# Conditioned attention on one core: one head's softmax sums in two chunks move from ScalarE to VectorE, one addition of q's corner block from VectorE to GpSimd

## The chip, the cores and the metric

The kernel runs on one core of a Trainium2 chip. The core has five engines that run side by side: TensorE (PE in the profile, PEld for its weight loads), VectorE (DVE), ScalarE (ACT), GpSimd (POOL) and SyncE (SP), which issues most transfers. Each engine works through its own instructions in program order and waits at semaphores for the others. The metric is the device time of one execution in microseconds (us), the median of several; lower is better.

## The reference

The input x has 8 sequences of 512 rows and 512 columns, with one conditioning row for each sequence. Attention has 16 heads of 32 columns:

```python
Q = split(x @ Wq.T + bq); K = split(x @ Wk.T + bk); V = split(x @ Wv.T + bv)
cQ = Q + split(cond @ Wq.T + bq)
cK = K + split(cond @ Wk.T + bk)
scores = einsum('bhqd,bhkd->bhqk', cQ, cK) / sqrt(32)
attn = softmax(scores, axis=-1)
out  = x + merge(einsum('bhqk,bhkd->bhqd', attn, V))
```

Everything is float32. The softmax needs, for each head and query row, the maximum of its 512 scores, the exponentials, and their sum.

## The kernel before

**Tiles and steps.** A tile t is one sequence and four heads: 8 sequences by 4 groups make T = 32 tiles. The main loop `for t in range(1, T - 3)` takes one tile a step, and each step has four items, in this order: "V" (i = 0), "q" (1), "k" (2) and "v" (3). A 512-row sequence is cut into four query chunks of 128, numbered qc.

Two tiles are always under way. The softmax of tile t + 1 is prepared in step t: its row scores for chunk 1, 2 and 3 in items V, q and k, and chunk 0 of tile t + 2 in item v (`rows`). In item V, `weighted` multiplies the exponentials of tile t - 1 with V. In items q, k and v, `products` computes a quarter of the next sequence's q, k or v projections.

**Odd and even tiles.** Tiles 1, 3, ..., 27 are in the list `BLOCKED`. For an odd tile the exponentials are computed once, with queries in the partitions, kept in `arena` (`rows_kept`), exchanged between partitions by transfers (`exchange`, L677, some issued by GpSimd, the others by SyncE) and turned by VectorE (`turn_blocks`, L666). For an even tile they are computed twice: once in the PSUM banks only for the sums (`denominators`, L693), and once more in the other orientation (`exponentials`, L749 to L763). So an even step has, in each item, four exponentials by L763 for tile t and four by L693 for tile t + 1, which is odd. An odd step has L693 alone. The exponential of L693 subtracts the row maximum, which it gets as a bias (`nmax`, from VectorE, L602 and L655), and returns the sum of its row in `sums`. In the profile this is a second instruction, ACTIVATION_READ_ACCUMULATOR, behind the ACTIVATE. Later `masked` (L801, GpSimd) spreads the sums for the division in `weighted`.

**The projections** use seven products instead of eight for a 2 by 2 block scheme. An odd step calls `four_products`, an even step `three_products`; each writes to two PSUM banks, `one_` and `two_`. The results of a pair of tiles lie in `c1` (with its second half `c12`) and `c2` (with its second half `c22`). In the odd step, ScalarE takes the four products out of PSUM (L540, L542, L543; L527 and L532 for v) and GpSimd adds them up (L544, L545). In the even step VectorE adds the other three in three operations (L556, L557, L558). `c12` is the corner block: it gets two products there, the others one each.

**The order of the work** is written out by hand (`manual_schedule`): each engine's order is the order of the program. The eight PSUM banks change their roles at every item; `begin` and `released` keep a list of them by the time at which they come free. In an even step the exponentials of an item take the first four, the row scores the last four. So the row scores (L646) of item k go to the two banks of heads 2 and 3 of item q's sums, which L693 frees, and to `one_` and `two_` of item q, which L557 and L558 free. Those of item v stand in the same way to item k. SyncE's and GpSimd's transfers are issued at the places that `ORDERS` names.

Of the kernel before, what the change touches and what calls it, by code (L numbers as in the profile page):

```python
# [11 lines left out]
AF = mybir.ActivationFunctionType  # L12
ALU = mybir.AluOpType
AX = mybir.AxisListType
# [3 lines left out]
def kernel(  # L18
# [38 lines left out]
    nc = tc.nc  # L57
    P = 128
# [10 lines left out]
    HS = S // 2  # L69
# [2 lines left out]
    EARLY = 3  # L72
    SINGLY = "qk"
    BY_POOL = (3,)
    WARM = (48, 4)
    BLOCKED = list(range(1, T - 4, 2))

# [44 lines left out]
    def banks(i, n=1):  # L122

        row = row_of[0] or [at_end[j] for j in TURNS[turn[0]]]
        j = row[i]
        if n == 1:
            return psum[:, j, :]
        k = row[i + 1]
        return psum[:, j : k + 1 : k - j, :]
# [14 lines left out]
    def released(*roles):  # L144
        order[:] = [row_of[0][i] for i in roles]
# [76 lines left out]
    def rows_kept(t, half):  # L222

        a = arena[:, half * HG : (half + 1) * HG, :]
        return a.rearrange("p g (c h s) -> p g c h s", c=2, h=HG)
# [104 lines left out]
    def in_place(b):  # L330
# [5 lines left out]
    wT = {  # L336
        n: const.tile([P, NC, D], F32, tag=f"wT{n}", name=f"wT_{n}") for n in ("q", "k", "v")
    }
# [63 lines left out]
    def pair_of(t, n):  # L402

        if (n, t // 2) not in pairs:
            pairs[n, t // 2] = qkp.tile([P, 2, S], F32, tag=n, name=f"{n}T_{t // 2}")
        return pairs[n, t // 2]
# [66 lines left out]
    def twice(a):  # L473
        return a.unsqueeze(1).broadcast_to([P, 2, HS])

    def halves(a):
        return a.rearrange("p (h s) -> p h s", h=2)


    def parts_of(n, b, u):  # L480

        if n == "v":
            v = vs[b % 2]
            return v[:, u::2, :HS], v[:, u + 2, :HS], v[:, u::2, HS:], v[:, u + 2, HS:]
        o = pair_of(b * G + u * 2, n)
        return halves(o[:, 0, :]), o[:, 0, HS:], halves(o[:, 1, :]), o[:, 1, HS:]

    def plus(n, b, u, g, o, pt, rest):

        if n == "v":  # L490
            nc.vector.tensor_tensor(o, pt, rest, ALU.add)
        else:
            add = tok[:, "qk".index(n), u * 2 + g, b : b + 1]
            nc.vector.scalar_tensor_tensor(o, pt, add, rest, ALU.add, ALU.add)

    def first_products(n, b, u, dens, small, at, first=0, held=None):
# [17 lines left out]
        nc.vector.tensor_tensor(c1[:, 0, :], two_[:, HS:], m1, ALU.add)  # L514
        plus(n, b, u, 1, c22, one_[:, HS:], c12)

    def four_products(n, b, u, dens, small, at):

        one_, two_ = banks(at), banks(at + 1)
        c1, c12, c2, c22 = parts_of(n, b, u)  # L520
        m1 = c2[:, 0, :]
        if n == "v":
            v = vs[b % 2].rearrange("p c (two f) -> p (c two) f", two=2)
            product(n, b, u, 1, one_[:, :HS])
            product(n, b, u, 6, one_[:, HS:])
            dens(range(EARLY))
            nc.scalar.copy(v[:, u * 2 + 1 : u * 2 + 5 : 3, :], halves(one_))  # L527
            dens(range(EARLY, HG))
            small()
            product(n, b, u, 2, two_[:, :HS])  # L530
            product(n, b, u, 7, two_[:, HS:])
            nc.scalar.copy(v[:, u * 2 : u * 2 + 6 : 5, :], halves(two_))  # L532
        else:
            dens()
            product(n, b, u, 1, one_[:, :HS])
            product(n, b, u, 6, two_[:, HS:])
            small()
            product(n, b, u, 2, two_[:, :HS])
            product(n, b, u, 7, one_[:, HS:])
            nc.scalar.copy(m1, one_[:, :HS])  # L540
            i = "qk".index(n)
            nc.scalar.activation(c1, halves(two_), AF.Identity, bias=tok[:, i, u * 2, b : b + 1])  # L542
            nc.scalar.activation(c22, one_[:, HS:], AF.Identity, bias=apart_tok[:, i, u, b : b + 1])  # L543
        nc.gpsimd.tensor_tensor(c1, c1, twice(m1), ALU.add)  # L544
        nc.gpsimd.tensor_tensor(c22, c22, c12, ALU.add)  # L545

    def three_products(n, b, u, dens, small, at):

        dens()
        one_, two_ = banks(at[0]), banks(at[1])  # L550
        product(n, b, u, 5, one_[:, HS:])
        product(n, b, u, 4, one_[:, :HS])
        small()
        product(n, b, u, 3, two_[:, :HS])
        c1, c12, c2, c22 = parts_of(n, b, u)
        nc.vector.tensor_tensor(c12, one_[:, HS:], c12, ALU.add)  # L556
        nc.vector.tensor_tensor(c2, halves(one_), twice(c22), ALU.add)  # L557
        nc.vector.tensor_tensor(c12, two_[:, :HS], c12, ALU.add)  # L558
        if n != "v":
            for g in range(2):  # L560
                qkT[n, b * G + u * 2 + g] = pair_of(b * G + u * 2, n)[:, g, :]
# [32 lines left out]
    sums = {}  # L594
# [73 lines left out]
    def exchange(t, half):  # L668
# [3 lines left out]
        for g in range(HG):  # L672
            for a in range(HG):
                queue = nc.gpsimd if a in BY_POOL else nc.sync
                of = arena[a * BL : (a + 1) * BL, half * HG + g, :]
# [3 lines left out]
    def denominators(t, qc, w=HG, js=range(HG)):  # L679

        if t >= T - 2:
            return
        for j in js:
            if t in BLOCKED:
                to = rows_kept(t, qc // 2)[:, :, qc % 2, j, :].rearrange(
                    "p g (c e) -> p g c e", e=BL
                )
            else:
                to = banks(w + j)
            of = banks(w + j)  # L690
            if t in BLOCKED:
                of = of.rearrange("p (c g e) -> p g c e", g=HG, e=BL)
            nc.scalar.activation(  # L693
                to,
                of,
                AF.Exp,
                bias=nmax[t][:, qc, j, :],
                accum_out=sums[t][:, qc, j, :],
            )

    def split_max(t, on=nc.gpsimd):

# [169 lines left out]
    apart_tok = const.tile([P, 2, NC // 2, B], F32, tag="aparttok", name="aparttok")  # L872
# [39 lines left out]

    keep_warm(WARM[0])
    bank = bank_of
# [22 lines left out]
    project(0, "k", pk, two[0])  # L937
    keep_warm(WARM[1])
    turn_first_x(1)
# [174 lines left out]
    def turn_more(t, i):  # L1114

        for u in (t - 1, t, t + 1):
            if u in BLOCKED and (t - u, i) in TURNED:
                n = turned.get(u, 0)
                turned[u] = n + TURNED[t - u, i]
                turn_blocks(u, range(n, turned[u]))  # L1120

    ORDERS = {
        (1, 0): [],
        (1, 1): ["store", "x"],
# [8 lines left out]
    for t in range(1, T - 3):  # L1133
        b, r = divmod(t, G)
        blocks = t in BLOCKED
        w = 0 if blocks else HG
        items = ["V", "q", "k", "v"]
        for i, item in enumerate(items):
            rows = (t + 1, i + 1) if i < 3 else (t + 2, 0)
            begin(w)  # L1140
            if not blocks:
                exponentials(t, i)
            late_first = item in ("v" if blocks else "qkv") and t % 2 == 1
            hold = row_max(*rows, late_first, w, not blocks and item in SINGLY)

            def held(i=i, hold=hold):
                hold()
                if i == 2:
                    split_max(t + 1)
                    turn_max(t + 1)  # L1150

            dens = lambda js=range(HG): denominators(*rows, w, js)
            if item in "qkv":
                products(t, item, blocks, held, dens, nothing)
            else:
                held()
                dens()
                if blocks:
                    weighted(t - 1, banks(4), banks(5), nothing)
                    released(6, 7, 0, 1, 2, 3, 5, 4)  # L1160
                else:
                    weighted(t - 1, banks(0), banks(1), nothing)
                    released(2, 3, 1, 4, 5, 6, 7, 0)
            if i == 0 and r % 2 == 0:
                turn_x(t + NC + 2)
                turn_x(t + NC + 3)
            if i == 0 and r == 1:
                combine_x(b + 1, 1, nc.gpsimd)
            if i == 1 and r == 0:
                combine_x(b + 1, 0, nc.gpsimd)  # L1170
            if i == 2:
                aparts[t] = masked(t)
            turn_more(t, i)
            for what in ORDERS[t % 2, i]:
                if what == "store":
                    store()
                elif what == "residual":
                    if 3 < t + 1 <= T - 4:
                        load_residual(t + 1)
                elif what == "x":  # L1180
                    load_pairs()
                elif t + 1 in BLOCKED:
                    exchange(t + 1, what)
# [67 lines left out]
    t = T - 3  # L1251
# [25 lines left out]
    t = T - 2  # L1277
# [25 lines left out]
    t = T - 1  # L1303
# [61 lines left out]
    b, g = divmod(t, G)  # L1365
# [55 lines left out]
```

## Time and profile before

| | |
|---|---|
| median of 3 runs | 660.53 us (660.41 to 660.67) |
| the profiled execution | 660.98 us, span 658.9 us |
| TensorE's granted clock | 1.00 |
| PE busy | 651.5 us, 99% of the span |
| VectorE busy | 574.6 us, 87% |
| ScalarE busy | 542.5 us, 82% |
| GpSimd busy | 336.8 us, 51% |
| one odd and one even step in the middle | 18.58 + 20.46 us |

The span runs from the first to the last instruction of the execution that was profiled; that execution's own time is 2 us longer. Busy times of one engine are sums over its instructions. A matmul that waits for a semaphore after the one before it has begun may show as a gap, or only as a group of matmuls that takes longer than its like, because matmuls overlap and their ends are modelled. Rows of the order of time give the start in us from the span's beginning, the length, engine, line, operation, output and input, shapes and count, and in brackets how long the engine stood idle before and what ended that. "PEld" rows are weight loads, which run ahead of their matmuls.

### The profile page before, as it was taken

What the parts mean: (1) busy time and instruction counts of PE and PEld (TensorE: products, weight loads), DVE (VectorE), ACT (ScalarE), POOL (GpSimd) and SP (SyncE); (2) the same over time, 40 slices, a digit from 0 to 9 for tenths busy, and PEclk for the clock granted to TensorE, in tenths of its full rate; (3) what the DMA queues carried; (4) which work ended last, traced back from release to release, by engine and by line L of the source; (5) the groups of instructions that cost most, each with busy time, mean ns of one, the idle gap of its engine ahead of it and who ended that gap; (6) DMA issues with size and microseconds to landing.
All of it is one profiled execution on the core that took longest, in us unless ns stands there. A gap on an engine that the chain in (4) does not pass through costs nothing.

```text
span 658.9 us, 23947 instructions
## 1 busy us (share of the span) xinstructions
PE 651.5 (99%) x9568; PEld 304.1 (46%) x9568; DVE 574.6 (87%) x844; ACT 542.5 (82%) x1393; POOL 336.8 (51%) x446
## 2 busy tenths in 40 slices
PE   8999999999999999999999999999999999999997
PEld 7444443544535454444445444454553544444432
DVE  4898989989798898979989898898979888897886
ACT  2579798888989888898989979788897988889664
POOL 5552543647537464466635664464753646444340
PEclk9999999999999999999999999999999999999999
DMA  9718548385675838657484875839567582940212
GB/s 205 144 44 214 118 109 210 67 220 122 153 172 121 209 74 214 149 130 194 94 214 97 191 155 131 210 71 217 118 164 166 115 205 48 223 106 4 56 33 33
DMA packets 140818, 90.91 MB, mean 138 GB/s; under 512 B 117436, under 2 KB 126308, under 8 KB 140708
## 3 DMA queue, kind: packets, MB, share of 16 engines
q1 hardware_dynamic: 133252, 73.91, 49.0%
q0 software_dynamic: 5568, 14.95, 8.8%
q8 instruction: 75, 1.23, 0.8%
q10 hardware_dynamic: 1888, 0.52, 0.4%
q14 instruction: 35, 0.29, 0.1%
HBM read 20.27 MB, written 8.39 MB: 43 GB/s over the span
## 4 chain that ended last, share of the span: by engine, by line
PE 95%; POOL 2%; DVE 1%; DMA 1%; issue 0%; ACT 0%; ACTq 0%; DVEq 0%; POOLq 0%
PE psum L469 43%; PE psum L774 17%; PE psum L646 10%; PE psum L638 9%; PE psum L752 8%; PE psum L749 3%; PE psum L410 2%; DMA early<-in_x_dram 1%; PE psum L1227 1%; PE psum L1340 0%; PE psum L811 0%; ACT psum L693 0%; POOL wc_q L364 0%; POOL wc_q L361 0%; POOL wc_k L362 0%
## 5 line engine op out<-in xcount | busy, mean ns | idle before, releaser
L602 DVE TENSOR_REDUCE nmax<-psum 128x1 f32<-128x512 f32 x326 | 204.9, 680 | 41.7 <-PE psum L646 38.2
L693 ACT ACTIVATE psum<-psum,nmax 128x512 f32<-128x512 f32 x256 | 169.2, 665 | 46.5 <-DVE nmax L602 34.3
L763 ACT ACTIVATE arena<-psum 128x512 f32<-128x512 f32 x264 | 136.3, 603 | 29.3 <-PE psum L752 21.7
L693 ACT ACTIVATE arena<-psum,nmax 128x512 f32<-128x512 f32 x224 | 152.8, 709 | 5.8 <-issue 4.4
L666 DVE STREAM_TRANSPOSE blocks<-blocks 128x1024 f32<-128x1024 f32 x112 | 132.2, 1218 | 0.2 <-issue 0.2
L655 DVE TENSOR_REDUCE nmax<-psum 128x2 f32<-128x1024 f32 x87 | 105.3, 1212 | 1.1 <-PE psum L646 1.1
L842 POOL TENSOR_TENSOR res<-res,recs 128x512 f32<-128x512 f32 x30 | 31.4, 1048 | 121.1 <-DVE res L841 121.1
L677 POOL DMA_DIRECT2D blocks<-arena x112 | 55.9, 504 | 72.3 <-ACT arena L693 63.5
L646 PE MATMUL psum<-kT,qT 32*128 32x512 f32 x576 | 87.9, 604 | 0.0
L774 PE MATMUL psum<-arena,v 128*32 128x512 f32 x576 | 68.5, 597 | 0.0
L752 PE MATMUL psum<-qT,kT 32*128 32x512 f32 x528 | 67.9, 587 | 0.0
L638 PE MATMUL psum<-kT,qT 32*64 32x512 f32 x896 | 62.4, 613 | 0.0
L646 PEld LDWEIGHTS psum<-kT,qT 32*128 32x128 f32 x576 | 37.6, 182 | 34.1 <-DVE kT L558 6.5
L693 ACT ACTIVATION_READ_ACCUMULATOR psum<-psum,nmax 128x1 f32 x256 | 52.4, 205 | 0.0
L774 PE MATMUL psum<-blocks,v 128*32 128x256 f32 x896 | 52.1, 381 | 0.0
L693 ACT ACTIVATION_READ_ACCUMULATOR arena<-psum,nmax 128x1 f32 x224 | 50.9, 227 | 0.0
L843 POOL TENSOR_TENSOR xr<-res,xr 128x512 f32<-128x512 f32 x30 | 38.4, 1281 | 2.4
L209 POOL TENSOR_TENSOR xr<-xr,wT_q 128x512 f32<-128x512 f32 x30 | 38.3, 1280 | 0.3
L774 PEld LDWEIGHTS psum<-blocks,v 128*32 128x32 f32 x896 | 26.3, 110 | 25.0 <-ACT arena L763 10.6
L841 DVE STREAM_TRANSPOSE res<-psum 128x512 f32<-128x512 f32 x28 | 20.1, 717 | 19.0 <-issue 16.0
L469 PE MATMUL psum<-wT_v,xT 128*32 128x256 f32 x512 | 34.2, 382 | 0.0
L469 PE MATMUL psum<-wc_v,xc 128*32 128x256 f32 x512 | 33.5, 379 | 0.0
(194 smaller groups left out, 1012.3 us busy)
## 6 DMA issues: line engine op xcount, KB each, us to landing
blocks<-arena SPq DMA_DIRECT2D x336, 128.0 KB, 4.1
blocks<-arena POOLq DMA_DIRECT2D x112, 128.0 KB, 4.0
xr<-in_x_dram SPq DMA_DIRECT2D x60, 128.0 KB, 2.8
x<-in_x_dram SPq DMA_DIRECT2D x56, 128.0 KB, 2.8
out_dram<-xr SPq DMA_DIRECT2D x56, 128.0 KB, 2.3
w_q<-in_L_cond_Wq_dram SPq DMA_DIRECT2D x4, 256.0 KB
w_k<-in_L_cond_Wk_dram SPq DMA_DIRECT2D x4, 256.0 KB, 8.2
w_v<-in_L_cond_Wv_dram SPq DMA_DIRECT2D x4, 256.0 KB
```

The lines of the kernel that those rows point to most:

```text
L469: nc.tensor.matmul(pt[r], still[:, r], moving, start=(kc == kcs[0]), stop=(kc == kcs[-1]))
L602: nc.vector.tensor_reduce(nmax[t][:, qc, j : j + 1, 0], pt, AX.X, ALU.max, negate=True)
L638: nc.tensor.matmul(pt[i * n : (i + 1) * n], qkT["q", t][r, qc * P + i * n : qc * P + (i + 1) * n], qkT["k", t][r, :], start=True, stop=True,)
L646: nc.tensor.matmul(pt, qkT["q", t][r, qc * P : (qc + 1) * P], qkT["k", t][r, :], start=True, stop=True,)
L655: nc.vector.tensor_reduce(nmax[t][:, qc, pr * 2 : pr * 2 + 2, 0], pt, AX.X, ALU.max, negate=True)
L666: nc.vector.transpose(e, e)
L677: queue.dma_start(to.rearrange("p c h s -> p (c h s)"), of)
L693: nc.scalar.activation(to, of, AF.Exp, bias=nmax[t][:, qc, j, :], accum_out=sums[t][:, qc, j, :],)
L752: nc.tensor.matmul(bank[j], qkT["k", t][r, kc * P : (kc + 1) * P], qkT["q", t][r, :], start=False, stop=True,)
L763: nc.scalar.activation(e[:, i, :], bank[pr * 2 + i], AF.Exp)
L774: nc.tensor.matmul(pt[j * HD : (j + 1) * HD, at], vs[b % 2][:, kc, (g * HG + j) * HD : (g * HG + j + 1) * HD], e, start=(kc == chunks[0]), ...
L843: nc.gpsimd.tensor_tensor(xr[t], y, xr[t], ALU.add)
```

## The change

Two things are done, both in the main loop.

First, `BY_VECTOR` names head 0 in chunks 2 and 3. For odd tiles from 3 on, the exponential of that head and chunk (L693) is issued without its sum. A new function, `sums_by_vector`, adds the row up with a VectorE reduction over the 512 exponentials in the arena. It reads them as four pieces of 128 a row. It is called at the end of items q (chunk 2) and k (chunk 3) of the even steps, behind VectorE's work on the item's products (`SUMMED`). These are 13 even steps and 26 reductions.

Second, for q alone (`HELPED`), the corner block is summed in another order. In the odd step ScalarE writes its term for the corner to an unused part of q's weight buffer (`room_beside`, two pieces of 128 columns a row) instead of `c22`, and GpSimd's addition writes the sum to `c12` instead of `c22`. In the even step VectorE computes `c2` first, then the third product minus that term into the weight buffer, and GpSimd adds `c22` to it. So VectorE has two operations there instead of three, and GpSimd one more: 14 even steps. The sum is the same.

TensorE's and SyncE's instructions and their order stay as they were.

```diff
+    BY_VECTOR = {2:(0,),3:(0,)}
+    HELPED = "q"
...
+    def room_beside(n):
+        a = wT["q" if n == "q" else "k"][:, 0:2, 3 * P :]
+        return a if n in HELPED else None
+
+    def split_of(a):
+        return a.rearrange("p (c s) -> p c s", c=2)
...
-            nc.scalar.activation(c22, one_[:, HS:], AF.Identity, bias=apart_tok[:, i, u, b : b + 1])
+            nc.scalar.activation(
+                beside if n in HELPED else c22,
+                split_of(one_[:, HS:]) if n in HELPED else one_[:, HS:],
+                AF.Identity,
+                bias=apart_tok[:, i, u, b : b + 1],
+            )
         nc.gpsimd.tensor_tensor(c1, c1, twice(m1), ALU.add)
-        nc.gpsimd.tensor_tensor(c22, c22, c12, ALU.add)
+        if n in HELPED:
+            nc.gpsimd.tensor_tensor(split_of(c12), beside, split_of(c12), ALU.add)
+        else:
+            nc.gpsimd.tensor_tensor(c22, c22, c12, ALU.add)
...
-        nc.vector.tensor_tensor(c12, one_[:, HS:], c12, ALU.add)
-        nc.vector.tensor_tensor(c2, halves(one_), twice(c22), ALU.add)
-        nc.vector.tensor_tensor(c12, two_[:, :HS], c12, ALU.add)
+        if n in HELPED:
+            beside = room_beside(n)
+            nc.vector.tensor_tensor(c2, halves(one_), twice(c12), ALU.add)
+            nc.vector.tensor_tensor(beside, split_of(two_[:, :HS]), beside, ALU.subtract)
+            nc.gpsimd.tensor_tensor(split_of(c12), beside, split_of(c22), ALU.add)
+        else:
+            nc.vector.tensor_tensor(c12, one_[:, HS:], c12, ALU.add)
+            nc.vector.tensor_tensor(c2, halves(one_), twice(c22), ALU.add)
+            nc.vector.tensor_tensor(c12, two_[:, :HS], c12, ALU.add)
...
+            by_scalar = t not in BLOCKED or t == 1 or j not in BY_VECTOR.get(qc, ())
             nc.scalar.activation(
...
-                accum_out=sums[t][:, qc, j, :],
+                **({"accum_out": sums[t][:, qc, j, :]} if by_scalar else {}),
             )
+
+    def sums_by_vector(t, qc):
+
+        if t in BLOCKED:
+            for j in BY_VECTOR[qc]:
+                nc.vector.tensor_reduce(
+                    sums[t][:, qc, j, :],
+                    rows_kept(t, qc // 2)[:, :, qc % 2, j, :],
+                    AX.XY,
+                    ALU.add,
+                )
...
+    SUMMED = {1:[2],2:[3]}
...
             turn_more(t, i)
+            if not blocks:
+                for qc in SUMMED.get(i, ()):
+                    sums_by_vector(t + 1, qc)
```

More of the change, by code (lines that the diff above doesn't have):

```diff
@@ L555, in three_products @@
         c1, c12, c2, c22 = parts_of(n, b, u)
-        nc.vector.tensor_tensor(c12, one_[:, HS:], c12, ALU.add)
-        nc.vector.tensor_tensor(c2, halves(one_), twice(c22), ALU.add)
-        nc.vector.tensor_tensor(c12, two_[:, :HS], c12, ALU.add)
+        if n in HELPED:
+            beside = room_beside(n)
+            nc.vector.tensor_tensor(c2, halves(one_), twice(c12), ALU.add)
[5 more added lines that the diff above has]
+            nc.vector.tensor_tensor(c12, two_[:, :HS], c12, ALU.add)
         if n != "v":
```

## The prediction

> **What bounds the kernel now.** I read the page's first and fourth parts, then the chain that ended last inside one pair of steps, the busy times of that pair item by item, and the order of time of ACT, PE's weight loads, DVE and POOL there. The profiled execution took 660.98 us with a span of 658.9; the median of the runs is 660.53, 0.07% less. All savings below are so small that they carry over to the median as they are.
>
> ```profile
> span 658.9 us, 23947 instructions
> PE 651.5 (99%) x9568; PEld 304.1 (46%) x9568; DVE 574.6 (87%) x844; ACT 542.5 (82%) x1393; POOL 336.8 (51%) x446
> PE 95%; POOL 2%; DVE 1%; DMA 1%; issue 0%; ACT 0%; ACTq 0%; DVEq 0%; POOLq 0%
> ```
>
> PE is busy throughout and holds 95% of the chain. So freeing DVE, ACT or POOL is worth only what PE loses by waiting for them, and a busy PE can hide such a wait in a matmul that begins late. It shows in one pair of steps, cut into the odd step and the even step's items V, q, k, v (columns: PE, PEld, DVE, ACT, POOL busy, then clock, DMA share, GB/s):
>
> ```profile
> 221.32:239.90 18.58, 18.58 (x300) 7.86 (x304) 18.16 (x24) 15.07 (x42) 10.11 (x13) 1.00 0.69 165
> 239.90:245.74 5.84, 5.84 (x97) 3.00 (x100) 4.84 (x7) 5.53 (x14) 3.25 (x3) 1.00 0.09 18
> 245.74:250.51 4.77, 4.77 (x72) 2.37 (x76) 4.60 (x8) 3.88 (x11) 3.77 (x5) 1.00 0.48 106
> 250.51:255.59 5.08, 5.08 (x73) 2.54 (x76) 4.05 (x9) 5.04 (x14) 0.80 (x3) 1.00 0.97 250
> 255.59:260.36 4.77, 4.77 (x77) 2.29 (x78) 3.44 (x7) 4.37 (x13) 3.28 (x5) 1.00 0.89 206
> ```
>
> Items q, k and v give PE the same matmuls, yet k takes 5.08 us and the others 4.77. The chain says where (start, length, what):
>
> ```profile
> 246.93 0.86 PE psum L646 x8
> 251.70 1.17 PE psum L646 x8
> 256.78 0.86 PE psum L646 x8
> ...
> 95.45 1.16 PE psum L646 x8
> 564.37 1.17 PE psum L646 x8
> ```
>
> The row scores (L646) of item k take 1.17 instead of 0.86: 0.31 us lost in every even step from t = 2 (95.45) to t = 26 (564.37), 13 steps. Who holds them:
>
> ```profile
> 251.73 0.19 PEld L646 LDWEIGHTS psum<-kT,qT 32*128 32x128 f32 x2
> ...
> 251.14 0.41 DVE L558 TENSOR_TENSOR qT<-psum,qT 128x256 f32<-128x256 f32 x1
> ...
> 246.95 2.06 ACT L763 ACTIVATE arena<-psum 128x512 f32<-128x512 f32 x4 [0.89 <-PE psum L752]
> 248.88 0.71 ACT L693 ACTIVATE arena<-psum,nmax 128x512 f32<-128x512 f32 x1
> ...
> 250.20 0.72 ACT L693 ACTIVATE arena<-psum,nmax 128x512 f32<-128x512 f32 x1
> 250.77 0.25 ACT L693 ACTIVATION_READ_ACCUMULATOR arena<-psum,nmax 128x1 f32 x1
> 250.86 0.73 ACT L693 ACTIVATE arena<-psum,nmax 128x512 f32<-128x512 f32 x1
> 251.43 0.25 ACT L693 ACTIVATION_READ_ACCUMULATOR arena<-psum,nmax 128x1 f32 x1
> 251.72 2.06 ACT L763 ACTIVATE arena<-psum 128x512 f32<-128x512 f32 x4
> 253.65 0.71 ACT L693 ACTIVATE arena<-psum,nmax 128x512 f32<-128x512 f32 x1
> ```
>
> Two heads' weights are loaded at 251.73, 0.05 after ACT's last sum of item q was read out (251.43 + 0.25 = 251.68). That instruction frees the bank. In this step, DVE's last addition of q had ended at 251.55. So the loss is ACT's: its row of eight exponentials, begun when PE's L752 let it (246.95), ends 4.73 later, and PE's unstalled item is 4.77.
>
> **The change part by part.**
>
> *ACT, 13 x 2 sums dropped.* For head 0 in items q and k the exponential no longer returns its sum, so one read-out goes. A read-out starts 0.57 after its exponential and the next exponential 0.09 after that: a pitch of 0.66 (250.20 to 250.86). Without the read-out the trace has no such exponential. The nearest is L542, also 128x512 with a bias from a buffer:
>
> ```profile
> 274.84 0.71 ACT L542 ACTIVATE kT<-psum,tok 128x512 f32<-128x512 f32 x1
> 275.42 0.49 ACT L543 ACTIVATE kT<-psum,aparttok 128x256 f32<-128x256 f32 x1
> ```
>
> Its successor starts 0.58 later. So the drop saves 0.66 - 0.58 = 0.08, or 0.09 if the successor starts where the read-out did. The other end: L763, an exponential without such a bias, has a pitch of (four from 251.72, then L693 at 253.65) 0.48, which would save 0.18. I take 0.085, since the bias stays. The lower end is zero, if ACT then waits for the maxima instead (under DVE).
>
> The Trainium skill ("ScalarE: Activation LUTs", section "What ACT_TABLE_LOAD costs") gives a 512-column activation with a pointer bias about 707 ns and lets neighbours overlap by about 93, a pitch of 0.61; by that estimate the drop saves 0.05 a time and the sum below would be 0.6 us. The length agrees with L542's 0.71, the overlap does not (0.71 - 0.58 = 0.13), so I go by the row.
>
> *Where that goes.* k's wait falls from 0.31 to about 0.22. Then v begins 0.085 earlier, and k's own ACT row must be done 0.085 earlier too, or the loss reappears in v. The rows of v:
>
> ```profile
> 256.20 0.25 ACT L693 ACTIVATION_READ_ACCUMULATOR arena<-psum,nmax 128x1 f32 x1
> 256.38 0.31 PEld L646 LDWEIGHTS psum<-kT,qT 32*128 32x128 f32 x4 [0.43 <-DVE kT L558]
> ```
>
> The last of the four loads ends at 256.69 and, at some 0.18 a load (two took 0.19 above), starts at 256.51, just after k's last read-out (256.45), and v's L646 takes its 0.86: the load arrives in time with nothing to spare. Because chunk 3 is dropped in k as well, ACT keeps pace and v stays unstalled. Dropping it in q alone would be worth nothing. DVE frees v's first banks with k's L558, load at 256.38; the latest load still in time was 256.51, so 0.13 - 0.085 leaves 0.04. Gain: 0.085 per pair, 13 pairs, 1.1 us.
>
> *DVE, 26 sums added, 14 additions of 128x256 taken away.*
>
> ```profile
> L602 DVE TENSOR_REDUCE nmax<-psum 128x1 f32<-128x512 f32 x326 | 204.9, 680 | 41.7 <-PE psum L646 38.2
> ...
> 250.21 0.42 DVE L556 TENSOR_TENSOR qT<-psum,qT 128x256 f32<-128x256 f32 x1
> 250.54 0.68 DVE L557 TENSOR_TENSOR qT<-psum,qT 128x512 f32<-128x512 f32 x1
> ...
> 252.58 2.48 DVE L602 TENSOR_REDUCE nmax<-psum 128x1 f32<-128x512 f32 x4 [1.03 <-PE psum L646]
> 255.91 0.41 DVE L558 TENSOR_TENSOR kT<-psum,kT 128x256 f32<-128x256 f32 x1
> 257.66 1.29 DVE L602 TENSOR_REDUCE nmax<-psum 128x1 f32<-128x512 f32 x2 [1.33 <-PE psum L646]
> ```
>
> A sum over 512 elements should cost what L602's maximum over 512 does, 0.68: 26 x 0.68 = 17.7 us of work more, 14 x 0.41 = 5.7 less. Both sums fall in pockets in which DVE waits for PE. In q the three additions become two, ending at 250.21 + 0.60 + 0.41 = 251.22 instead of 251.55; the sum runs from 251.15 to 251.83, and the next work is at 252.58. In k it runs from 256.25 to 256.93; the next is at 257.66, or 257.57 with the gain. q's exponential for head 0 ended at 248.88 + 0.71 = 249.59, so the sum waits for nothing. The maxima stay ahead of ACT: k's second ends at 252.58 + 0.60 + 0.68 = 253.86, its exponential would start at 253.65 + 0.58 = 254.23. With the cover gone it would cost: past 1.43 us in q or 1.32 in k, the next maxima are late. The odd step, where DVE is busy 18.16 of 18.58, gets no sum.
>
> *q's banks freed earlier, 0.33 us.* L557's bank is freed at 250.89 and L558's at 251.22. Worth nothing alone: ACT's 251.68, later 251.60, still ends last.
>
> *POOL, 14 additions of 128x256; ACT's term into the weight buffer.*
>
> ```profile
> 237.87 0.73 POOL L545 TENSOR_TENSOR kT<-kT 128x256 f32<-128x256 f32 x1
> 249.01 2.00 POOL L677 DMA_DIRECT2D blocks<-arena  x4
> 251.02 0.30 POOL L801 TENSOR_TENSOR wT_k<-sums,which 128x64 f32<-128x64 f32 x1
> 256.75 2.00 POOL L677 DMA_DIRECT2D blocks<-arena  x4 [5.42 <-ACT arena L693]
> ```
>
> At 0.73 each it runs from about 251.28 to 252.01. Behind it on POOL stands the masking of the sums (0.30) and then four transfers that wait until 256.75: 5.42 us of cover, in every second pair shared with two additions of combine_x. The queue of SP is passed by nothing new. The finished corner is first read an odd step later. In odd steps the same instructions run, with another place to write and read; the rows show no reason for another length. Cost nothing.
>
> *Not in the sum:*
>
> ```profile
> 245.86 0.72 DVE L841 STREAM_TRANSPOSE res<-psum 128x512 f32<-128x512 f32 x1 [1.12 <-issue]
> 519.51 0.72 DVE L841 STREAM_TRANSPOSE res<-psum 128x512 f32<-128x512 f32 x1 [1.47 <-issue]
> ```
>
> At t = 24 one DVE transpose began 0.35 us later than its like, and q's scores behind it waited; whether such a late start stays, goes or comes twice I can't derive.
>
> Sum: 660.5 - 1.1 = 659.4 us (span 657.8), 0.17% less.
>
> **The rivals.** *The exponential without its sum goes at L763's pitch.* Saved 0.18 a time; then k's L558, with 0.13 of room in v, holds v's loads for 0.05 to 0.06, and 0.12 per pair stay: 1.6 us, 659.0. For it: nothing but the shared function. Against: L542, with its bias, has 0.58.
>
> *The stall only moves into v.* v's loads have no reserve on ACT and 0.04 on DVE. If k's row of exponentials doesn't shorten with q's, or k's additions come 0.1 late, v loses what k gains: 660.5. Against: both engines' rows in k start from PE's events, which don't move.
>
> *The sums outgrow their pockets (slower).* The sum reads four strided pieces of 128 from the arena. If it took three maxima, 2.05 us, it would end at 253.20 in q, 0.62 late; k's additions would hold v for 0.62 - 0.04 = 0.58, less the 0.085 gained: 13 x 0.5 = 6.5 us, 667 or more. It decides from about 1.4 us on. For it: no row of a strided reduction exists. Against: L655's reduction over two banks,
>
> ```profile
> L655 DVE TENSOR_REDUCE nmax<-psum 128x2 f32<-128x1024 f32 x87 | 105.3, 1212 | 1.1 <-PE psum L646 1.1
> ```
>
> costs 1.21 for 1024, so pieces are nearly free.
>
> **How the numbers follow.** What a measurement can tell from no change is 0.2%, 1.3 us: 659.2 and 661.9. The forecast gets 0.62, with a range of its own of 659.0 (0.09 a time and the single 0.35 gone) to 659.9 (0.05 a time); 0.28 of it lies below 659.2 and 0.34 above. The faster rival gets 0.12, the moved stall 0.16, the slower one, with late DVE starts as at t = 24 in several more pairs, 0.10. That makes faster 0.40, same 0.50, slower 0.10. The range leaves the slower rival out: 658.8, just under the faster rival, to 660.7, just over the moved stall.
>
> **What would show it.** Right: item k at about 4.99 instead of 5.08, L646 there at about 1.08, V, q and v as before, a pair of 38.95 instead of 39.04; the pitch behind head 0 at 0.57 to 0.58; the sums at 0.65 to 0.70 with the waits in front of the maxima shortened from 1.03 and 1.33 by as much. Wrong: v's L646 above 0.86, sums over 1.3 us, or an L646 in k that falls by much more than 0.09, which would mean that the bank's last holder isn't ACT.

## The result

| | median | runs | ratio to the kernel before |
|---|---|---|---|
| before | 660.53 us | 11 | |
| with the change | 659.26 us | 11 | 0.998 (95% interval 0.9972 to 0.9988) |

The change saves 1.27 us, 0.19%. That was predicted as 1.1 us. The profiled execution of the changed kernel took 659.31 us, its span is 657.5.

In the changed kernel's numbering L626 is the maximum that was L602, L670 the row scores that were L646, L718 the exponential with a bias (L693), L799 the one without (L763), L730 the new sum, L576 and L577 VectorE's two operations on q, L578 GpSimd's new addition. L580 to L582 are VectorE's three additions on k that were L556 to L558, L662 the odd step's row scores (L638), L679 the maximum over two banks (L655). L542 is now the last copy of v (it was L532); the L542 of the prediction has become L552.

The other engines' totals moved as the added and removed operations say. PE's busy time fell with the span, from 651.5 to 650.2, so its share stayed at 99%:

```profile
span 657.5 us, 23947 instructions
PE 650.2 (99%) x9568; PEld 303.8 (46%) x9568; DVE 584.9 (89%) x856; ACT 540.1 (82%) x1367; POOL 346.1 (53%) x460
```

DVE works 10.3 us more, ACT 2.4 less, POOL 9.3 more. (By the lengths of the rows in the prediction DVE would have had 17.7 - 5.7 = 12.0 more. Most of the difference is overlap: an operation starts some 0.08 before the one in front of it ends, as the rows below show.) Where the gain comes from is not to be seen there. It shows in the even step's items V, q, k and v of the pair that the prediction read:

```profile
239.36:245.20 5.84, 5.84 (x96) 3.00 (x100) 4.84 (x7) 5.53 (x14) 3.25 (x3) 1.00 0.10 20
245.20:249.97 4.77, 4.77 (x72) 2.37 (x76) 4.61 (x8) 3.88 (x10) 3.78 (x5) 1.00 0.48 107
249.97:254.96 4.99, 4.99 (x72) 2.47 (x76) 4.22 (x9) 4.86 (x13) 1.47 (x4) 1.00 0.95 253
254.96:259.73 4.77, 4.77 (x76) 2.21 (x79) 4.12 (x8) 4.37 (x13) 3.29 (x5) 1.00 0.88 209
```

Item k went from 5.08 to 4.99, and V, q and v kept their lengths. The chain names the matmuls, the row scores of items q, k and v:

```profile
246.38 0.86 PE psum L670 x8
...
251.15 1.07 PE psum L670 x8
...
256.14 0.86 PE psum L670 x8
```

1.17 became 1.07 in k, and nothing came back in v. ScalarE's rows in item q show the cause (order of time; two exponentials of one line that follow each other without a read-out between them are one row):

```profile
248.33 1.29 ACT L718 ACTIVATE arena<-psum,nmax 128x512 f32<-128x512 f32 x2
249.47 0.24 ACT L718 ACTIVATION_READ_ACCUMULATOR arena<-psum,nmax 128x1 f32 x1
249.56 0.73 ACT L718 ACTIVATE arena<-psum,nmax 128x512 f32<-128x512 f32 x1
250.13 0.25 ACT L718 ACTIVATION_READ_ACCUMULATOR arena<-psum,nmax 128x1 f32 x1
250.22 0.73 ACT L718 ACTIVATE arena<-psum,nmax 128x512 f32<-128x512 f32 x1
250.79 0.25 ACT L718 ACTIVATION_READ_ACCUMULATOR arena<-psum,nmax 128x1 f32 x1
```

Two exponentials take 1.29 together: the second, 0.72 long, starts 0.57 behind the first, where the read-out used to start. The others keep their 0.66.

VectorE's rows from item q's additions to item v's maxima, and GpSimd's beside it:

```profile
249.67 0.68 DVE L576 TENSOR_TENSOR qT<-psum,qT 128x512 f32<-128x512 f32 x1
250.26 0.41 DVE L577 TENSOR_TENSOR wT_q<-psum,wT_q 128x256 f32<-128x256 f32 x1
250.60 0.67 DVE L730 TENSOR_REDUCE sums<-arena 128x1 f32<-128x512 f32 x1
252.04 2.48 DVE L626 TENSOR_REDUCE nmax<-psum 128x1 f32<-128x512 f32 x4 [0.77 <-PE psum L670]
...
255.37 0.41 DVE L582 TENSOR_TENSOR kT<-psum,kT 128x256 f32<-128x256 f32 x1
255.70 0.67 DVE L730 TENSOR_REDUCE sums<-arena 128x1 f32<-128x512 f32 x1
257.03 1.29 DVE L626 TENSOR_REDUCE nmax<-psum 128x1 f32<-128x512 f32 x2 [0.66 <-PE psum L670]
```

```profile
250.76 0.72 POOL L578 TENSOR_TENSOR qT<-wT_q,qT 128x256 f32<-128x256 f32 x1 [0.29 <-DVE wT_q L577]
251.45 0.29 POOL L837 TENSOR_TENSOR wT_k<-sums,which 128x64 f32<-128x64 f32 x1
256.11 2.00 POOL L701 DMA_DIRECT2D blocks<-arena  x4 [4.38 <-ACT arena L718]
```

Both sums lie in the pockets: behind them VectorE still waits 0.77 and 0.66 us for PE. GpSimd's wait in front of its transfers is 4.38 instead of 5.42. Neither is on the path.

### The profile page after: what moved, and what is told of

It reads as the page before. It is cut to its first block, busy times and chain, and to the rows that moved or that the text cites. A ratio compares the mean times of both kernels' runs of the same rounds, so it can differ in the third digit from the quotient of the medians.

```text
span 657.5 us, 23947 instructions
## 1 busy us (share of the span) xinstructions
PE 650.2 (99%) x9568; PEld 303.8 (46%) x9568; DVE 584.9 (89%) x856; ACT 540.1 (82%) x1367; POOL 346.1 (53%) x460
## 4 chain that ended last, share of the span: by engine, by line
PE 94%; POOL 3%; DVE 1%; DMA 1%; issue 0%; ACT 0%; DVEq 0%; POOLq 0%
PE psum L471 43%; PE psum L810 18%; PE psum L670 10%; PE psum L662 9%; PE psum L788 9%; PE psum L785 3%; PE psum L412 1%; PE psum L1267 1%; DMA early<-in_L_cond_Wk_dram 1%; PE psum L1380 0%; POOL early L248 0%; PE psum L847 0%; POOL early L290 0%; ACT psum L718 0%; POOL wc_q L363 0%
## 5 line engine op out<-in xcount | busy, mean ns | idle before, releaser
L626 DVE TENSOR_REDUCE nmax<-psum 128x1 f32<-128x512 f32 x326 | 204.7, 679 | 29.9 <-PE psum L670 26.2
L718 ACT ACTIVATE psum<-psum,nmax 128x512 f32<-128x512 f32 x256 | 169.2, 665 | 46.7 <-DVE nmax L626 34.5
L799 ACT ACTIVATE arena<-psum 128x512 f32<-128x512 f32 x264 | 136.3, 603 | 30.2 <-PE psum L788 21.2
L718 ACT ACTIVATE arena<-psum,nmax 128x512 f32<-128x512 f32 x224 | 150.3, 709 | 5.9 <-issue 4.3
L679 DVE TENSOR_REDUCE nmax<-psum 128x2 f32<-128x1024 f32 x87 | 105.3, 1211 | 1.1 <-PE psum L670 1.1
L670 PE MATMUL psum<-kT,qT 32*128 32x512 f32 x576 | 86.7, 600 | 0.0
L662 PE MATMUL psum<-kT,qT 32*64 32x512 f32 x896 | 62.4, 613 | 0.0
L718 ACT ACTIVATION_READ_ACCUMULATOR psum<-psum,nmax 128x1 f32 x256 | 52.6, 205 | 0.0
L670 PEld LDWEIGHTS psum<-kT,qT 32*128 32x128 f32 x576 | 37.3, 182 | 33.1 <-issue 7.5
L718 ACT ACTIVATION_READ_ACCUMULATOR arena<-psum,nmax 128x1 f32 x198 | 44.9, 227 | 0.0
```

Source lines behind the costliest of these rows:

```text
L626: nc.vector.tensor_reduce(nmax[t][:, qc, j : j + 1, 0], pt, AX.X, ALU.max, negate=True)
L662: nc.tensor.matmul(pt[i * n : (i + 1) * n], qkT["q", t][r, qc * P + i * n : qc * P + (i + 1) * n], qkT["k", t][r, :], start=True, stop=True,)
L670: nc.tensor.matmul(pt, qkT["q", t][r, qc * P : (qc + 1) * P], qkT["k", t][r, :], start=True, stop=True,)
L679: nc.vector.tensor_reduce(nmax[t][:, qc, pr * 2 : pr * 2 + 2, 0], pt, AX.X, ALU.max, negate=True)
L718: nc.scalar.activation(to, of, AF.Exp, bias=nmax[t][:, qc, j, :], **({"accum_out": sums[t][:, qc, j, :]} if by_scalar else {}),)
L799: nc.scalar.activation(e[:, i, :], bank[pr * 2 + i], AF.Exp)
```

## The experiments

Below, the length of a pair of steps is the time from the first matmul of one odd step to that of the next (median of the twelve pairs from t = 4 on). It is a sharper reading than the run times: the time up to the first pair differed between 63.9 and 65.7 us from one profile to another, and the runs of one kernel spread over 0.6 to 1.8 us. Each median is of 5 to 11 runs, that of the three sums of 2 alone. Before, a pair is 39.04, with the change 38.95. The pair at t = 2 is told apart, because its banks lie differently.

The length of a group of row scores is given in two ways. In the chain it counts from where the work before it ended: 1.17 for k before the change. "From first to last matmul" counts from the start of the group's first matmul, which overlaps with the work before it: 1.33 for the same group.

| kernel | pair | pair at t = 2 | median, us | ratio (95% interval) |
|---|---|---|---|---|
| before | 39.04 | 39.15 | 660.4 to 660.5 | |
| the change | 38.95 | 38.98 | 659.26 | 0.998 (0.9972 to 0.9988) |
| sums alone | 38.95 | 39.15 | 658.82 | 0.9973 (0.9963 to 0.9984) |
| corner alone | 39.04 | 39.07 | 659.77 | 0.9988 (0.9979 to 0.9997) |
| chunk 2 only | 39.04 | 39.07 | 660.21 | 0.9995 (0.9986 to 1.0004) |
| chunk 3 only | 39.04 | 39.07 | 660.29 | 0.9994 (0.9985 to 1.0003) |
| sums twice | 38.96 | 38.99 | 658.90 | 0.9975 (0.9966 to 0.9985) |
| sums three times | 39.89 | 39.54 | 671.28 | 1.0162 (1.0144 to 1.0181) |
| two heads | 38.94 | 38.97 | 658.66 | 0.9970 (0.9960 to 0.9981) |
| two heads, no corner | 39.00 | 39.15 | 660.27 | 0.9998 (0.9989 to 1.0007) |
| chunk 0 too, head 0 | 38.90 | 38.93 | 658.50 | 0.9966 (0.9953 to 0.9978) |
| chunk 0 too, head 3 | 38.87 | 38.90 | 657.82 | 0.9962 (0.9950 to 0.9975) |
| chunk 0's head 3 and two heads | 38.85 | 38.88 | 657.60 | 0.9957 (0.9943 to 0.9970) |

### The two halves of the change, each alone

```diff
-    HELPED = "q"
+    HELPED = ""
```

> The change with the sums moved to VectorE, but q's corner block added up as before (three VectorE operations in item q). Theory ACT (the dropped read-outs alone make the gain): item k's row scores take 1.24 us as in the changed kernel, a pair of steps 38.95, about 659.4. Rival BANKS (q's banks must be freed earlier for the gain to come): item k's row scores stay at 1.33, a pair 39.04, about 660.5. Rival SHARED (each half of the change brings part): 1.28 and 39.00, about 660.

Measured: a pair 38.95, row scores of k 1.24 from first to last matmul, 658.82 us.

```diff
-    BY_VECTOR = {2:(0,),3:(0,)}
+    BY_VECTOR = {}
...
-    SUMMED = {1:[2],2:[3]}
+    SUMMED = {}
```

> The change with q's corner block moved, and all sums returned by ScalarE as before. Theory ACT: nothing, a pair stays at 39.04 and item k's row scores at 1.33, 660.5; only the pair at t = 2 may gain up to 0.08. Rival BANKS: 38.95, 659.3. Rival SHARED: 39.00, about 660.

Measured: a pair 39.04, row scores of k 1.33, but 39.07 instead of 39.15 at t = 2.

So the sums make the whole repeating gain. The corner's earlier banks bring 0.08 us once, at t = 2. The medians of the runs don't follow the pairs so closely: that of the corner alone is 0.7 us below the kernel before, that of the sums alone 1.7, where their pairs give 0.1 and 1.1. Between the two profiled executions of the corner alone and of the kernel before, 0.08 is the pair at t = 2, 0.33 a late start that only the one before has (below), and 0.40 the time up to the first pair. So it is not shown that the 0.7 is a gain of the corner's move, and what the medians differ by beyond the pairs stays unexplained.

### One of the two chunks

```diff
-    BY_VECTOR = {2:(0,),3:(0,)}
+    BY_VECTOR = {2:(0,)}
...
-    SUMMED = {1:[2],2:[3]}
+    SUMMED = {1:[2]}
```

> The change with only chunk 2's sum on VectorE (item q); chunk 3's is returned by ScalarE again. Theory PAIRED (v has no reserve on ACT, so the stall moves): item k's row scores 1.24, item v's 0.95 in the chain (1.11 with the last matmul's tail) in place of 0.86 (1.03), a pair 39.04, 660.5. Rival HALF (each drop brings half): v's stay at 0.86, a pair at 38.95 to 39.00, 659.3 to 660.

The chain of this run, row scores of items k and v:

```profile
251.15 1.07 PE psum L670 x8
...
256.14 0.94 PE psum L670 x8
```

k is as short as in the change, and v now takes 0.94 instead of 0.86. A pair is 39.04: the stall has moved from k to v, whole.

```diff
-    BY_VECTOR = {2:(0,),3:(0,)}
+    BY_VECTOR = {3:(0,)}
...
-    SUMMED = {1:[2],2:[3]}
+    SUMMED = {2:[3]}
```

> The change with only chunk 3's sum on VectorE (item k); chunk 2's is returned by ScalarE again. Theory PAIRED: item k's row scores stay at 1.33 from first to last matmul, v's at 1.03, a pair 39.04, 660.5; ACT is 0.09 ahead in v, for nothing. Rival HALF: a pair at 39.00, 660.

```profile
250.57 1.17 PE psum L670 x8
...
255.65 0.86 PE psum L670 x8
```

Nothing gained: 39.04. Each drop alone (both runs keep the corner's move) is worth nothing in a pair from t = 4 on, both together 0.09. That settles the central step of the prediction.

### How much room VectorE has

```diff
-                    sums_by_vector(t + 1, qc)
+                    for _ in range(2):
+                        sums_by_vector(t + 1, qc)
```

> The changed kernel with each of VectorE's 26 sums made twice (the second writes the same result again). Theory POCKET (VectorE's waits for PE behind the sums, 0.77 us left in q and 0.65 in k, hide the work up to their size): one sum more takes 0.59, so nothing is lost, a pair 38.95, time as the changed kernel's. Rival BUSY (VectorE at 89% is close to the bound, each sum is paid): 2 x 0.59 a pair, 40.1, 674.

```profile
250.17 1.40 DVE L730 TENSOR_REDUCE sums<-arena 128x1 f32<-128x512 f32 x2
251.62 2.48 DVE L626 TENSOR_REDUCE nmax<-psum 128x1 f32<-128x512 f32 x4
```

Measured: a pair 38.96, 0.01 above the change, and 658.90 us. VectorE's busy time is 602.3 us instead of 584.9, 1.3 more in each of the 13 pairs. The two sums into one output take 1.40, so the second costs 0.73 and not the 0.59 that was expected. With that the pocket in q is just full: no wait for PE is listed in front of the maxima any more, and the same holds in k.

And three times:

```diff
-                    sums_by_vector(t + 1, qc)
+                    for _ in range(3):
+                        sums_by_vector(t + 1, qc)
```

> The changed kernel with each of the 26 sums made three times. Theory POCKET: two sums more take 1.18, so item k's maxima start 0.41 late, k's last addition too, and v's row scores, with 0.04 of room, take 0.37 more (1.40 from first to last matmul); v's maxima come 0.5 late on top. A pair 39.3 to 39.7, 664 to 669. Rival BUSY: 2.36 a pair, 41.3, 690. Rival HIDDEN (VectorE never sets the time): 38.95.

Measured: a pair 39.89 and 671.28 us, more than the 39.3 to 39.7 and 664 to 669 that were expected. The direction was right and the size too small. The maxima behind the sums of q, and the chain from item v's row scores into the odd step (L662 there):

```profile
253.70 2.12 DVE L730 TENSOR_REDUCE sums<-arena 128x1 f32<-128x512 f32 x3
255.73 2.47 DVE L626 TENSOR_REDUCE nmax<-psum 128x1 f32<-128x512 f32 x4
...
259.52 1.14 PE psum L670 x8
...
263.39 1.41 PE psum L662 x16
...
268.43 1.24 PE psum L662 x16
273.32 1.04 PE psum L662 x16
```

From the start of q's sums to k's maxima it is 2.03 us here and 1.44 in the change (250.60 to 252.04): the maxima are 0.59 late, not 0.41, because each sum more costs about 0.72 instead of 0.59. Item v loses as much: from the end of k's row scores to the end of v's it is 5.34 us (median of the pairs) instead of 4.77, and v's first row score starts only behind VectorE's last addition of k. From there to the end of V's row scores in the odd step it is 4.13 instead of 3.77. 0.57 + 0.36 are the 0.93 us of a pair. The loss in item q of the odd step, 1.24 for 1.04 above, belongs to three of the thirteen pairs, which take 40.13 to 40.15. ScalarE waits for late maxima in the odd step:

```profile
262.19 0.66 ACT L718 ACTIVATE psum<-psum,nmax 128x512 f32<-128x512 f32 x1 [0.81 <-DVE nmax L626]
...
267.10 0.66 ACT L718 ACTIVATE psum<-psum,nmax 128x512 f32<-128x512 f32 x1 [1.79 <-DVE nmax L626]
```

In the change the first of the two does not wait, and the second waits 1.52:

```profile
258.14 0.70 ACT L718 ACTIVATE psum<-psum,nmax 128x512 f32<-128x512 f32 x1
...
262.47 0.66 ACT L718 ACTIVATE psum<-psum,nmax 128x512 f32<-128x512 f32 x1 [1.52 <-DVE nmax L626]
```

In the odd step VectorE has little room to catch up in, as the row of that step before the change shows (18.16 of 18.58 busy). The expectation had counted on the lateness of v's maxima; what it had too small was the price of a repeated sum.

### Two heads

```diff
-    BY_VECTOR = {2:(0,),3:(0,)}
+    BY_VECTOR = {2:(0,1),3:(0,1)}
```

> The changed kernel with two heads' sums (0 and 1) on VectorE in chunks 2 and 3. Theory ACT WITH VECTORE'S LIMIT: k's row scores 1.15 instead of 1.24; v would begin 0.18 earlier than in the kernel before, but k's last addition leaves 0.13, so v's take 1.08 instead of 1.03; a pair 38.90, about 0.6 us less than the changed kernel. Rival ACT ALONE: v's stay at 1.03, a pair 38.86, 1.2 us less. Rival FULL POCKETS (two sums no longer fit): a pair of 39 or more.

```profile
250.83 0.99 PE psum L670 x8
...
255.73 0.92 PE psum L670 x8
```

k falls by another 0.08, v rises by 0.06: a pair 38.94, 0.02 below the change where 0.05 were expected. The limit is where it was placed, at VectorE's last addition of k, and it bites by 0.01 more:

```profile
255.51 0.31 PEld L670 LDWEIGHTS psum<-kT,qT 32*128 32x128 f32 x8 [0.61 <-DVE kT L582]
```

v's weight loads waited for that addition, which ended at 255.46; ScalarE's last sum of k had been read out at 255.41.

The same without the corner's move:

```diff
-    BY_VECTOR = {2:(0,),3:(0,)}
-    HELPED = "q"
+    BY_VECTOR = {2:(0,1),3:(0,1)}
+    HELPED = ""
```

> Two heads' sums (0 and 1) on VectorE in chunks 2 and 3, with q's corner block added up as before the change. Theory POCKET: without the corner's move VectorE has 0.44 left behind the first sum in q, the second takes 0.59, so k's maxima and k's last addition come 0.15 late, and v's row scores take 1.24 instead of 1.09: a pair 39.08, 660.5. So the corner's move is worth its 0.33 us once there are two sums. Rival (the corner's move is worth nothing in any case): 38.94, 658.7.

```profile
252.56 1.27 DVE L730 TENSOR_REDUCE sums<-arena 128x1 f32<-128x512 f32 x2
253.75 2.48 DVE L626 TENSOR_REDUCE nmax<-psum 128x1 f32<-128x512 f32 x4
```

k's maxima start right behind the sums, with no wait for PE left, and a pair is 39.00. With the corner moved, two sums gave 38.94. So the corner's 0.33 us earlier is worth nothing with one sum and 0.06 a pair with two. 0.14 was expected. The miss is in the size of the pocket: one VectorE operation starts some 0.08 before the one in front of it ends (252.56 + 1.27 = 253.83 against 253.75), so of the lateness of 0.15 only half was there. Nor did it show where it was expected: v's row scores take 1.11 from first to last matmul, not 1.24, and k's 1.20 instead of 1.16. With two sums dropped, ScalarE's last read-out of q ends at 252.60 and VectorE's third addition of q at 252.65, so that here q's own bank, freed late, holds k by 0.05.

### A third drop, in another item

Item V's row scores take 0.99 where q's take 0.86, before and after the change. They wait for ScalarE's last copy of the odd step's item v (now L542), behind the exponentials of chunk 0: in the change it ends at 240.37, and the waiting weight loads start at 240.42.

```profile
240.55 0.99 PE psum L670 x8
```

```diff
-    BY_VECTOR = {2:(0,),3:(0,)}
+    BY_VECTOR = {0:(0,),2:(0,),3:(0,)}
...
                 dens()
+                if not blocks:
+                    sums_by_vector(t + 1, 0)
                 if blocks:
```

> The changed kernel with head 0's sum of chunk 0 on VectorE as well: ScalarE drops it in item v of the odd step, VectorE adds it up in item V of the even step, in front of the reciprocal, where it waited 1.12 us. Theory ACT: V's row scores wait for ScalarE's last copy of v in the odd step; they take 1.07 instead of 1.16, a pair 38.86, about 1.2 us less than the changed kernel. Rival PE (that copy starts by PE's products): V's stay at 1.16, a pair 38.95. Rival VECTORE: the transposition behind the sum comes late, q's row scores go above 1.03, no gain or a loss.

A pair is 38.90: half of the gain came. ScalarE in the odd step's item v:

```profile
236.74 1.35 ACT L718 ACTIVATE arena<-psum,nmax 128x512 f32<-128x512 f32 x2 [0.31 <-DVE nmax L626]
237.98 0.19 ACT L718 ACTIVATION_READ_ACCUMULATOR arena<-psum,nmax 128x1 f32 x1
```

Two exponentials in 1.35, not 1.29: the second started 0.66 behind the first although no read-out stood between. Its maximum came no earlier (it ended at 237.30, the exponential started at 237.40). So the drop was moved to head 3, whose maximum has long been there:

```diff
-    BY_VECTOR = {0:(0,),2:(0,),3:(0,)}
+    BY_VECTOR = {0:(3,),2:(0,),3:(0,)}
```

> The changed kernel with the sum of chunk 0 on VectorE for head 3 instead of head 0 (chunks 2 and 3 as in the changed kernel). Theory MAXIMUM (in the run with head 0 the exponential of head 1 started 0.66 behind head 0's, as with a read-out, because its maximum came no earlier; by head 3 the maxima are all there): the whole 0.09 arrives, V's row scores 1.07 instead of 1.10, a pair 38.86 to 38.87, 0.4 us less than with head 0. Rival PE (ScalarE's last copy of v waits for its products): V's stay at 1.10, a pair 38.90.

```profile
238.62 0.71 ACT L718 ACTIVATE arena<-psum,nmax 128x512 f32<-128x512 f32 x1
239.20 0.60 ACT L542 COPY v<-psum 128x512 f32<-128x512 f32 x1
```

The copy starts 0.58 behind the exponential, V's row scores take 1.07 (before 1.16, with head 0 1.10, from first to last matmul), and a pair 38.87, as expected.

Both together:

```diff
-    BY_VECTOR = {2:(0,),3:(0,)}
+    BY_VECTOR = {0:(3,),2:(0,1),3:(0,1)}
...
                 dens()
+                if not blocks:
+                    sums_by_vector(t + 1, 0)
                 if blocks:
```

> Chunk 0's head 3 and heads 0 and 1 of chunks 2 and 3 on VectorE. If the two gains are independent (they lie in items V and k): a pair 38.85, about 1.3 us below the changed kernel, 657.9. If the fuller VectorE (one late start more in the odd step) takes it back: 38.87 or more.

```profile
239.86 0.90 PE psum L670 x8
...
250.38 0.99 PE psum L670 x8
...
255.28 0.92 PE psum L670 x8
```

A pair 38.85 and 657.60 us, the lowest median of all: 0.9957 of the kernel before (0.9943 to 0.9970). In the pairs the two gains add up (0.08 and 0.02).

## Why the prediction was right

**The bound.** Right. The gain lies in row scores of item k that the busy share of PE can't show, and the engine that held them was ScalarE. The corner alone, which frees q's other banks 0.33 us earlier, changed nothing in a pair from t = 4 on.

**The price of a read-out.** 0.085 was taken; the exponential without it has its successor 0.57 behind, so it is 0.09. It was the row with a bias (the prediction's L542, 0.58) that told, not the one of the same function without (L763, 0.48). The rival with 0.18 is gone. The pitch of 0.61 that the prediction worked out from the figures of the Trainium skill ("ScalarE: Activation LUTs", section "What ACT_TABLE_LOAD costs") was too long: the trace has 0.57. The saving of 0.05 that the upper end of the range used shows in no run.

**Where it goes.** Right to the hundredth in k (4.99 and 1.07, against "about 4.99" and "about 1.08"), and v stayed at 0.86. That v has no reserve on ScalarE is shown by chunk 2 alone. That VectorE's last addition of k leaves little is shown by the two heads, which v's row scores repaid with 0.06 of 0.08.

**VectorE's pockets.** The sum took 0.67 (0.68 taken, from a maximum of the same width), and the waits left behind it 0.77 and 0.66 (0.75 and 0.64 by the prediction's times). A second sum fits, a third does not. The price of the slower rival was named as "667 or more" for a sum of three maxima's length, 0.5 a pair. With three sums it was 671: item v lost 0.57, and the lateness ran on into the odd step and took 0.36 more there. That rival's mechanism is real, and only its condition did not hold: a strided sum costs no more than a maximum.

**GpSimd.** 0.72 for 0.73, in idle time.

**The sum.** 13 pairs of 0.085 were 1.1 us. The profiles' 13 pairs together fell from 507.99 to 506.69, by 1.30: twelve by 0.09 and the one at t = 2 by 0.17. That last was left out by the prediction: at t = 2 the sums alone gain nothing (39.15) and the corner alone 0.08, and the two together 0.17. The traces show why. At t = 2 it is VectorE that holds v before the change: v's weight loads start at 100.33, 0.05 behind k's last addition (100.27), while ScalarE had finished at 100.21. So with the sums alone v loses what k gains: it takes 4.95 instead of 4.85 (from the end of k's row scores to the end of its own). With the corner moved it takes 4.78.

That the medians differ by 1.27, so close to 1.1, is in part luck: the medians of the two halves alone lie up to 0.6 beyond what their pairs give, so an agreement to 0.2 proves little. The mechanism rests on the items and the pairs.

**Not derived.** One late start of about 0.3 us is in the profile of before (t = 24) and one in that of the change, in another pair and item. Five of the other profiles have none (sums alone, corner alone, sums twice, both runs with chunk 0 and one head). Such starts would add to the scatter between runs; what causes them stays open.

## What to carry to other kernels

A saving on an engine that stands beside the bound is worth what the bound waits for it, item by item; where each item's slack is used up, as here, two consecutive items must both be shortened or the stall only moves. Look for such a wait as a group of matmuls that is longer than its like, since a busy share of 99% doesn't show it. Work can be laid for nothing into a pocket in which another engine waits, up to the pocket's length; past it, the lateness is paid, and it can run on into the items behind.

## What the runs showed of the hardware

A row's sum returned with an exponential is listed as an instruction of 0.19 to 0.26 us, but costs its engine only 0.09, as it overlaps with the next exponential (0.66 from start to start with it, 0.57 without). The bank, though, was released only when the read-out had ended: PE's waiting weight loads started 0.05 us behind that, not behind the exponential's end. A VectorE sum over four strided pieces of 128 from the arena took 0.672 to 0.676 us in 26 cases, no more than a maximum over 512 elements in a bank (0.68). A second sum into the same output started 0.71 behind the first (the run with the sums made twice), one into another output 0.59 (two heads).
